# Queries' sweep: the closing product moves from a bank of its own into a shared ring of two, and the transposes of tokens get a fourth bank

## The chip, the cores and the metric

The kernel runs on one core of one Trainium2 chip. The metric is device time in microseconds of one execution; of the kernel before three runs are shown, and one more execution was taken with a profile. Line numbers are those of the kernel before.

## The reference, cut to what matters

One transformer block over 2048 tokens of 1024 features, all in float32. The attention is over the 32 heads of one token, not over tokens.

```python
h = layernorm(x)                                  # 2048 x 1024
q, k, v = (h @ w.T + b for w, b in ((wq, bq), (wk, bk), (wv, bv)))   # as 32 heads of 32
probs = softmax(einsum('shd,std->sht', q, k) / sqrt(32))
x = x + einsum('sht,std->shd', probs, v).reshape(2048, 1024)
y = layernorm(x)
dq1, dq2, dq3 = (nf4_quant_dequant(w) for w in (w1, w2, w3))   # blocks of 64, 16 codes
x = x + (silu(y @ dq1.T) * (y @ dq2.T)) @ dq3.T   # hidden width 2752
```

## The kernel before, in words

The work goes in sweeps: queries (L531 to L560), keys (L623 to L641), values (L713 to L751), then the feed-forward part. Each of the first three projects the 2048 tokens in eight pairs of tiles of 128 tokens. A pair's projection, a product of 256 x 1024 by 1024 x 1024, is done by `products` (L348) with seven block products in place of eight (a scheme of the Strassen-Winograd kind): the left sides are four blocks of tokens (SA11, SA12, SA21, SA22) and four sums of them (S1 to S4, made on VectorE by `differences`, L394), the right sides four blocks of weights and their sums T1 to T4. Each block product is one call of `mm4` (L337): four float32 matmuls that the trace shows as eight rows, into one bank of PSUM.

PSUM has eight banks here. In the queries' sweep they are given out so:

- `z` and `q`, one bank each (pool ps_pj): running sums that several of the seven products add to, and that are copied out in between.
- a ring `x` of two banks (ps_pj, given by `bank`, L301): for `r`, the second product (L371), and for `ptw`, the transposes of weight tiles that `finish` (L147) makes when `flush` lets it go on (L157 to L163).
- `pt`, three banks (pool ps_t, L444): the transposes of token tiles, four transposes of 128 x 128 to a bank (L469 to L471). ScalarE copies each twice, once into A (L474) for the queries and keys, once into V (L475) for the values.
- `y`, one bank, in ps_t too (L385): the closing product, S4 by B22. The queries' sweep passes ps_t to `products` as `apart`; VectorE adds y to the copy u4 of z (L387). In the two later sweeps `apart` is None, and that product is added into z.

The order within a pair is: z and q begin (L362, L365), `fill(7)`, z again (L368), `fill(6)`, r (L372), `fill(2)`, z (L377), `fill(5)`, y (L386), `fill(3)`, q's second product (L389), `fill(4)`. The function `fill` (L539) puts other work between the products: in `fill(5)` the sixteen transposes of the next pair's two token tiles (`transposes`, L467), in `fill(7)` and `fill(3)` a step of a weight tile's transposes, and in each but `fill(5)` a step of the background. After the products a further `flush` follows, then `differences` for the next pair, the layout of the queries (`qk_T`, L401: a transpose and an add of the bias on VectorE) and a chunk of the sums of weights (`weight_chunk`, L509).

The background (L219) quantises the feed-forward weights to 4-bit codes and back: for a tile of weights a chain of fifteen steps, most of them a ScalarE activation `sg` (L242) and a VectorE operation on `r` (L243), with sixteen small scalings by block on ScalarE ahead of it and behind it (L195).

What sets the order: TensorE's instructions are run in the order of the program (L283 puts this engine alone under a schedule by hand). The instructions of VectorE, ScalarE, GpSimd and SyncE are put in order, when the kernel is built, by the framework's planner, from the dependencies, from costs that it assumes, and from the moments at which buffers come free in its plan. The bank that a new tile of a pool takes is chosen there too. On the chip each engine then follows its fixed order.

After the queries' sweep ps_t is closed (L560), and its four banks go to the scores of the keys' sweep (`ps_at`, L568).

Of the kernel before, what the change touches and what calls it, by code (L numbers as in the profile page):

```python
# [12 lines left out]
FP = mybir.dt.float32  # L13
# [3 lines left out]
PSUM = bass.MemoryType.PSUM  # L17

P = 128
# [12 lines left out]
TB = 512  # L32
# [37 lines left out]
def preln_block_kernel(  # L70
# [116 lines left out]
    def flush(steps=3):  # L187
        for _ in range(steps):
            if pending and next(pending[0], flush) is flush:
                pending.pop(0)  # L190
# [69 lines left out]
    def advance(n):  # L260
        for _ in range(n):
            next(bg, None)
# [13 lines left out]
    left, right = ExitStack(), ExitStack()  # L276
# [9 lines left out]
    SA11, SA12, SA22, S1, S2, S3, S4 = range(7)  # L286
# [14 lines left out]
    def bank(nm):  # L301
        pool, tag, bufs = hook["pool"]
        return pool.tile([P, TB], FP, tag=tag, name=nm, bufs=bufs)
# [15 lines left out]
    def load_W(m, name):  # L319
        src = block(m, *RAW[name]) if name in RAW else wtD[m, int(name[1])]  # L320
        nc.sync.dma_start(new_w(name), src)
# [15 lines left out]
    def mm4(dst, w, xop, start, stop):  # L337
        for k in range(4):
            nc.tensor.matmul(  # L339
                dst,  # L340
                w[:, k, :],
                xop[:, k, :],
                start=start and k == 0,
                stop=stop and k == 3,
                skip_group_check=True,
            )

    def products(A, fill, used=lambda name: None, apart=None):  # L348

        def mul(dst, a, w, start, stop):
            mm4(dst, A[:, a], W[w], start, stop)
            used(w)

        def copied(nm, src):
            t = pair.tile([P, TB], FP, tag=nm, name=nm)
            nc.scalar.copy(t, src)  # L358
            return t

        z = ps_pj.tile([P, TB], FP, tag="z", name="z")
        mul(z, SA11, "B11", True, False)  # L362
        g0 = copied("g0", z)
        q = ps_pj.tile([P, TB], FP, tag="q", name="q")
        mul(q, S3, "T3", True, False)  # L365
        s7 = copied("s7", q)
        fill(7)
        mul(z, S2, "T2", False, False)  # L368
        u2 = copied("u2", z)
        fill(6)  # L370
        r = bank("r")  # L371
        mul(r, SA12, "B21", True, True)  # L372
        ce = pair.tile([P, E], FP, tag="C0", name="ce")
        co = pair.tile([P, E], FP, tag="C1", name="co")
        nc.vector.tensor_tensor(ce[:, 0:512], g0, r, ALU.add)
        fill(2)
        mul(z, S1, "T1", False, apart is not None)  # L377
        u4 = copied("u4", z)
        nc.vector.tensor_tensor(co[:, 512:], u4, s7, ALU.add)
        fill(5)  # L380
        if apart is None:
            mul(z, S4, "B22", False, True)
            nc.scalar.copy(ce[:, 512:], z)
        else:
            y = apart.tile([P, TB], FP, tag="y", name="y", bufs=1)  # L385
            mul(y, S4, "B22", True, True)  # L386
            nc.vector.tensor_tensor(ce[:, 512:], u4, y, ALU.add)  # L387
        fill(3)
        mul(q, SA22, "T4", False, True)  # L389
        nc.vector.tensor_tensor(co[:, 0:512], u2, q, ALU.add)  # L390
        fill(4)
        return ce, co
# [8 lines left out]
    def qk_T(t, c, b):  # L401

        nc.vector.transpose(t, c.rearrange("p (h d) -> p h d", d=D))
        nc.vector.tensor_tensor(t, t, b.unsqueeze(2).to_broadcast([P, 32, 32]), ALU.add)
# [36 lines left out]

    sweep = ExitStack()
    work = sweep.enter_context(tc.tile_pool(name="workq", bufs=1, side="right"))
    ps_t = sweep.enter_context(tc.tile_pool(name="ps_t", bufs=3, space=PSUM, side="right"))  # L444

    xt = {}

    def load_x(i):
        xt[i] = work.tile([P, E], FP, tag="x", name="xt", bufs=2)
        nc.sync.dma_start(xt[i], xf[ts(i, P), :])  # L450
# [58 lines left out]
    def weight_chunk(m, k):  # L509

        b = {}
        for nm in ("B11", "B12", "B21", "B22"):
            b[nm] = work.tile([P, TB], FP, tag=f"c{nm}", name=f"c{nm}")
            nc.sync.dma_start(b[nm], block(m, int(nm[1]) - 1, int(nm[2]) - 1)[:, k, :])
        t3 = work.tile([P, TB], FP, tag="cT3", name="cT3")
        nc.vector.tensor_tensor(t3, b["B22"], b["B12"], ALU.subtract)
        nc.vector.tensor_tensor(b["B12"], b["B12"], b["B11"], ALU.subtract)
        nc.vector.tensor_tensor(b["B22"], b["B22"], b["B12"], ALU.subtract)
        nc.vector.tensor_tensor(b["B21"], b["B21"], b["B22"], ALU.subtract)
        for n, t in ((1, b["B12"]), (2, b["B22"]), (3, t3), (4, b["B21"])):  # L520
            nc.sync.dma_start(wtD[m, n][:, k, :], t)

    def next_W(m):
        return lambda name: load_W(m, name)

    def load_A(src, p):
        t = pair.tile([P, 7, 4, P], FP, tag="A", name="A", bufs=2)
        nc.sync.dma_start(t, src[p])
        return t

    for p in range(NP):  # L531
        more = p + 1 < NP
        now = nxt
        if more:
            load_x(2 * p + 2)
            load_x(2 * p + 3)
            nxt = Inputs(p + 1)

        def fill(n):  # L539
            if n in (7, 3):  # L540
                flush(1)
            if n == 5 and more:
                nxt.transposes(0)
                nxt.transposes(1)
            advance(0 if n == 5 else 1)

        cs = products(now.A, fill, (lambda name: None) if more else next_W("k"), ps_t)
        flush(1)
        if more:
            nxt.finished()  # L550
        for j in range(2):
            t = work.tile([P, 32, NH], FP, tag="qd", name="qd", bufs=2)
            qk_T(t, cs[j], qb_sb)
            nc.sync.dma_start(qD[2 * p + j], t)
        now.finished_v()
        weight_chunk("kv"[p // 4], p % 4)
        advance(2)
        if p == NP - 2:
            first = load_A(opD, 0)
# [3 lines left out]
    sweep, sweep_at = ExitStack(), ExitStack()  # L563
# [58 lines left out]
    A = first  # L622
    for p in range(NP):  # L623
        nextA = load_A(opD, p + 1) if p + 1 < NP else load_A(opV, 0)
        qd = load_tiles(qD, p, "ql", 3)

        def fill(n):
            if n in (7, 2, 5, 4):
                part()
            advance(1)  # L630
            if n in (3, 5):
                flush(1)

        cs = products(A, fill, (lambda name: None) if p + 1 < NP else next_W("v"))
        flush(1)
        for j in range(2):
            t = work.tile([P, 32, NH], FP, tag="kd", name="kd", bufs=3)
            qk_T(t, cs[j], kb_sb)
            parts.append(attend(2 * p + j, qd[j], t))
        advance(2)  # L640
        A = nextA  # L641
# [71 lines left out]
    for p in range(NP):  # L713
# [9 lines left out]
        def fill(n):  # L723
# [7 lines left out]
            if n == 3:  # L731
                if p == 0:
                    part()
                elif i + 1 in x1n:
                    keep_T(i + 1, x1n.pop(i + 1))

        cs = products(A, fill, (lambda name: None) if p + 1 < NP else next_op)
        flush(1)
        if p == 0:
            sweep.close()  # L740
            sweep = ExitStack()
# [9 lines left out]
        A = nextA  # L751
# [13 lines left out]
    def op(name, tbp):  # L765
        tag = "T1" if name == "B12" else name
        if ops.get(tag, (None, None))[:2] != (name, tbp):
            load_op(name, tbp)
        return ops[tag][2]
# [24 lines left out]
    def spent(us, finish=True):  # L794
        nonlocal owed
        owed += us * RATE
        n = int(owed)
        owed -= n
        if finish and step["n"] in range(5, 15):
            flush(1)  # L800
        advance(n)
# [75 lines left out]
    class Unit:  # L877


        A = {1: 0, 2: 1, 3: 6, 4: 2, 5: 3, 6: 4, 7: 5}  # L880
# [6 lines left out]
        def mul(self, n, dst, start, stop):  # L887
            mm4(dst, self.w[:, self.A[n]], op(self.B[n], self.tbp), start, stop)
            spent(3.43)
# [203 lines left out]
    now = Unit(*units.pop(0))  # L1093
    now.first()
    for n, (g, tbp) in enumerate(passes):
        half, sides = None, []
        while now is not None and now.tbp == tbp and now.c in g:
# [6 lines left out]
            if g[-1] == NFULL and unit.c == NFULL - 1:  # L1104
# [5 lines left out]
                now = None  # L1110
            if units:
                now = Unit(*units.pop(0))
                now.first()
            if unit.c < PAIRED and unit.c % 2:
                side = Sides(hs[unit.c - 1], n == 0, len(sides))
# [49 lines left out]
```

## Time and profile before

| What | us |
|---|---|
| median of three runs | 2488.63 |
| lowest and highest of them | 2483.4 and 2490.14 |
| profiled execution | 2493.61 |
| its span, first to last instruction | 2491.8 |
| TensorE busy in it | 2388.5 (96%) |
| VectorE busy | 1980.2 (79%) |
| ScalarE busy | 1611.2 (65%) |
| first product of the queries' sweep starts at | 12.8 |
| first product of the keys' sweep starts at | 248.6 |

The profile is of one execution. A group in it is a line of the kernel, an engine, an operation and the tile written and read; so "pt L471" is a transpose of tokens, "y L339" a matmul of the closing product (every block product has the line of `mm4`), and "V L475" ScalarE's copy for the values. Digits in tile names are left out, so A stands for the seven blocks and A21 alike, AV for the tile V and V for V21; wB and wT are weights, u stands for u2 and u4. The mean granted TensorE clock of the span is 0.985 of full speed.

### The profile page before, as it was taken

Reading aid. Unit: us, or ns where it says so; the run is one execution under the profiler, and the core shown is the slowest. Engines: PE = TensorE matmul, PEld = TensorE weight load, DVE = VectorE, ACT = ScalarE, POOL = GpSimd, SP = SyncE. Lnnn points to the kernel's source line nnn. Section 1 sums busy time; section 2 is a strip of 40 time slices with the busy share of each in tenths; the row PEclk is TensorE's granted clock in tenths of the full one; section 3 lists DMA queues with packets and bytes.
Section 4 is the critical chain, followed back from the end, with each engine's and each line's share of the span. In section 5 each row is a group of like instructions: output and inputs, shape, how many; then the busy total and the mean of one; then the engine's idle time right before and its main releaser. Section 6 shows DMA issues by size and latency. Waiting matters only on the chain.

```text
span 2491.8 us, 36722 instructions
## 1 busy us (share of the span) xinstructions
PE 2388.5 (96%) x14000; PEld 1119.1 (45%) x14000; DVE 1980.2 (79%) x2208; ACT 1611.2 (65%) x3267; POOL 278.6 (11%) x352
## 2 busy tenths in 40 slices
PE   7999999999899999999999999999999999999998
PEld 4444455545444444444444444444444444444433
DVE  7999788879988587889989799898988979871022
ACT  3556544344553378898888888889888888871200
POOL 1010000000000012030120301203012030120300
PEclk8999999999999999999999999999999999999998
DMA  8788643656669687394973949739396394862973
GB/s 309 282 313 315 243 156 123 232 211 220 208 230 313 205 287 168 118 191 153 321 171 118 191 147 302 195 110 203 144 301 162 144 198 148 289 153 72 202 269 131
DMA packets 177297, 513.90 MB, mean 206 GB/s; under 512 B 15904, under 2 KB 70176, under 8 KB 154720
## 3 DMA queue, kind: packets, MB, share of 16 engines
q1 hardware_dynamic: 136224, 438.08, 48.1%
q0 software_dynamic: 40320, 73.42, 18.2%
q8 instruction: 110, 1.80, 0.3%
q14 instruction: 67, 0.55, 0.1%
q10 hardware_dynamic: 576, 0.05, 0.0%
HBM read 283.69 MB, written 227.80 MB: 205 GB/s over the span
## 4 chain that ended last, share of the span: by engine, by line
issue 28%; PE 12%; ACT 10%; DVE 10%; DMA 7%; POOL 1%; SPq 0%; DVEq 0%; POOLq 0%; ACTq 0%
DVE r L243 7%; DMA x1d<-acc 5%; PE z L339 4%; ACT sg L242 3%; ACT wn L195 3%; PE z L989 2%; ACT acc L1002 2%; PE q L339 2%; ACT r L195 2%; PE y L989 1%; POOL x1d L1004 1%; PE rr L339 1%; DMA out_dram<-acc 1%; PE r L989 1%; DMA acc<-x1d 1%
## 5 line engine op out<-in xcount | busy, mean ns | idle before, releaser
L243 DVE SCALAR_TENSOR_TENSOR r<-sg,r 128x1024 f32<-128x1024 f32 x780 | 945.8, 1213 | 105.0 <-ACT sg L242 73.6
L242 ACT ACTIVATE sg<-wn 128x1024 f32<-128x1024 f32 x780 | 812.7, 1053 | 313.3 <-DVE r L243 299.2
L1004 POOL DMA_DIRECT2D x1d<-acc x280 | 243.3, 886 | 1283.4 <-ACT acc L1002 1137.3
L339 PE MATMUL z<-xB,w 128*128 128x512 f32 x720 | 323.8, 598 | 3.6 <-ACT u L909 1.9
L339 PE MATMUL z<-xT,w 128*128 128x512 f32 x656 | 295.9, 594 | 4.2 <-ACT u L902 4.2
L339 PE MATMUL q<-xT,w 128*128 128x512 f32 x656 | 291.6, 592 | 0.0
L195 ACT ACTIVATE wn<-wn,rc 128x64 f32<-128x64 f32 x1032 | 267.4, 340 | 22.4 <-DVE rc L215 22.4
L989 PE MATMUL z<-w,h 128*128 128x512 f32 x496 | 236.3, 605 | 21.7 <-ACT acc L1002 18.9
L339 PEld LDWEIGHTS z<-xB,w 128*128 128x128 f32 x720 | 135.0, 191 | 170.3 <-issue 153.8
L339 PEld LDWEIGHTS q<-xT,w 128*128 128x128 f32 x656 | 123.3, 190 | 149.5 <-issue 146.4
L339 PEld LDWEIGHTS z<-xT,w 128*128 128x128 f32 x656 | 122.0, 190 | 151.5 <-issue 138.7
L339 PE MATMUL z<-wT,A 128*128 128x512 f32 x384 | 178.1, 607 | 2.9 <-DVE wT L506 2.0
L339 PE MATMUL q<-wT,A 128*128 128x512 f32 x384 | 173.0, 593 | 1.6 <-DVE A L398 1.6
L339 PE MATMUL z<-wB,A 128*128 128x512 f32 x320 | 152.1, 620 | 13.1 <-ACT u L358 13.1
L195 ACT ACTIVATE r<-r,am 128x64 f32<-128x64 f32 x608 | 154.6, 341 | 13.8 <-DVE r L243 13.5
L989 PEld LDWEIGHTS z<-w,h 128*128 128x128 f32 x496 | 92.4, 192 | 138.6 <-issue 98.3
L989 PE MATMUL y<-w,h 128*128 128x512 f32 x320 | 149.9, 598 | 1.3 <-DVE h L968 1.1
L339 PE MATMUL rr<-xB,w 128*128 128x512 f32 x328 | 147.5, 592 | 0.0
L207 DVE TENSOR_REDUCE am<-wn 128x16 f32<-128x1024 f32 (+1 forms) x65 | 78.3, 1205 | 53.4 <-ACT r L195 47.5
L1002 ACT COPY acc<-z 128x512 f32<-128x512 f32 x160 | 92.8, 581 | 34.6 <-PE z L989 26.3
L339 PEld LDWEIGHTS q<-wT,A 128*128 128x128 f32 x384 | 71.9, 190 | 88.9 <-issue 83.0
L339 PEld LDWEIGHTS z<-wT,A 128*128 128x128 f32 x384 | 71.4, 192 | 83.2 <-issue 80.0
(132 smaller groups left out, 2592.1 us busy)
## 6 DMA issues: line engine op xcount, KB each, us to landing
x1d<-acc POOLq DMA_DIRECT2D x280, 256.0 KB, 6.3
wd<-wop SPq DMA_DIRECT2D x31, 2048.0 KB, 7.6
w<-wd SPq DMA_DIRECT2D x41, 1280.0 KB, 7.8
wn<-in_w_dram SPq DMA_DIRECT2D x63, 512.0 KB, 4.5
xT<-xdT SPq DMA_DIRECT2D x28, 1024.0 KB, 8.9
xB<-xdB SPq DMA_DIRECT2D x24, 1024.0 KB, 6.8
w<-wd SPq DMA_DIRECT2D x42, 512.0 KB, 4.8
w<-wd SPq DMA_DIRECT2D x10, 1536.0 KB, 7.2
```

Source lines behind the costliest of these rows:

```text
L195: nc.scalar.mul(dst[:, ts(n, BLOCK)], src[:, ts(n, BLOCK)], by[:, n : n + 1])
L207: nc.vector.tensor_reduce(am[:, :nb], v.rearrange("p (b e) -> p b e", e=BLOCK), AX.X, ALU.max, apply_absolute_value=True,)
L242: nc.scalar.activation(t, v, AF.Copy, bias=-edge * by, scale=by)
L243: nc.vector.scalar_tensor_tensor(r, t, code, r, ALU.min, ALU.max)
L339: nc.tensor.matmul(dst, w[:, k, :], xop[:, k, :], start=start and k == 0, stop=stop and k == 3, skip_group_check=True,)
L989: nc.tensor.matmul(dst, side[n][:, ts(q, P)], w3T[g[2 * m]][:, W3[n]], start=start and m == 0, stop=stop and m == 1, skip_group_check=True,)
L1002: nc.scalar.copy(t, src)
L1004: nc.gpsimd.dma_start(x1d[8 * tbp + 2 * q + j][n], t, accum_op=ALU.add)
```

## The change

In the queries' sweep the closing product `y` no longer has a bank of its own. It is taken from the ring of two by `bank("y")`, beside r and the weight tiles. The bank that this frees goes to the transposes of tokens: pool ps_t has four `pt` in place of three and no y. `apart` becomes a truth value. Nothing else is changed: the same instructions are issued, and TensorE's are issued in the same order.

```diff
-    def products(A, fill, used=lambda name: None, apart=None):
+    def products(A, fill, used=lambda name: None, apart=False):
...
-        mul(z, S1, "T1", False, apart is not None)
+        mul(z, S1, "T1", False, apart)
...
-        if apart is None:
+        if not apart:
             mul(z, S4, "B22", False, True)
             nc.scalar.copy(ce[:, 512:], z)
         else:
-            y = apart.tile([P, TB], FP, tag="y", name="y", bufs=1)
+            y = bank("y")
             mul(y, S4, "B22", True, True)
             nc.vector.tensor_tensor(ce[:, 512:], u4, y, ALU.add)
...
-    ps_t = sweep.enter_context(tc.tile_pool(name="ps_t", bufs=3, space=PSUM, side="right"))
+    ps_t = sweep.enter_context(tc.tile_pool(name="ps_t", bufs=4, space=PSUM, side="right"))
...
-        cs = products(now.A, fill, (lambda name: None) if more else next_W("k"), ps_t)
+        cs = products(now.A, fill, (lambda name: None) if more else next_W("k"), True)
```

## The prediction

> **What bounds the kernel now.** I first read the page: its busy line says PE 2388.5 of 2491.8 us (96%), so TensorE's own stream sets the end and about 103 us of it is idle. The slices tell where the second engine is full.
>
> ```profile
> PE   7999999999899999999999999999999999999998
> DVE  7999788879988587889989799898988979871022
> PEclk8999999999999999999999999999999999999998
> ```
>
> One slice is 62.3 us. The queries' sweep lies in slices 0 to 3 (12.8 to 248.6 us), and there DVE stands at 9 beside PE. So a wait taken off PE is worth its length only as far as DVE can follow. Second view: who PE waits for up to 260 us (columns: who waits, for whom, total us, times, longest).
>
> ```profile
> PE pt L471 <- ACT V L475: 11.9, 4, 4.2
> PE pt L471 <- DVE xn L334: 4.5, 1, 4.5
> ...
> PE pt L471 <- ACT AV L475: 1.0, 3, 0.3
> ```
>
> The seven waits on ACT's copies out of pt (first and third row) are 12.9 us: the fourth transpose tile of each pair has no bank until a copy empties one of the three. The xn wait is the start, and stays. Third view: PE in order of time, pair 1 and pair 3 (start, us, operation, idle before).
>
> ```profile
> 67.89 1.47 PE L471 MATMUL pt<-ident,xn 128*128 128x128 f32 x12
> 73.58 1.11 PE L471 MATMUL pt<-ident,xn 128*128 128x128 f32 x4 [4.21 <-ACT V L475]
> 74.49 6.10 PE L339 MATMUL y<-wB,A 128*128 128x512 f32 x8
> 80.42 3.60 PE L339 MATMUL q<-wT,A 128*128 128x512 f32 x8
> ...
> 129.22 1.47 PE L471 MATMUL pt<-ident,xn 128*128 128x128 f32 x12
> 131.04 0.65 PE L471 MATMUL pt<-ident,xn 128*128 128x128 f32 x4 [0.34 <-ACT AV L475]
> 131.53 3.60 PE L339 MATMUL y<-wB,A 128*128 128x512 f32 x8
> 134.97 3.60 PE L339 MATMUL q<-wT,A 128*128 128x512 f32 x8
> ```
>
> In pair 1 twelve transposes run, then 4.21 us of nothing, then the last four; and y after them takes 6.10 us where pair 3's takes 3.60. The pause also lowered the clock. Fourth view: stretches with the granted clock.
>
> ```profile
> 60.00:90.00 30.00, 25.79 (x66) 12.21 (x65) 26.69 (x39) 14.43 (x32) 4.04 (x6) 0.89 0.67 249
> ...
> 118.00:145.00 27.00, 26.66 (x78) 12.87 (x77) 26.93 (x39) 13.76 (x30) 3.03 (x4) 1.00 0.75 275
> 145.00:172.00 27.00, 26.66 (x78) 12.69 (x77) 27.00 (x38) 17.82 (x40) 1.77 (x4) 1.00 0.88 324
> ```
>
> Columns: stretch, length, busy us of PE, weight loads, DVE, ACT, POOL, then granted clock, DMA share, GB/s. In pairs 3 and 4, DVE is busy 26.93 and 27.00 of 27: no idle time at all. That is the number that decides this change.
>
> **What the fourth bank removes.** From the first transpose to the start of q's second product, the seven pairs that transpose take 10.66 (36.63 to 47.29), 12.53, 6.73, 5.75, 5.74, 5.75 and 11.17 us: 58.3 us. Without a wait it is 16 transposes at a pitch of 0.109 us (twelve take 1.47, the last 0.27) plus one product of 3.44 us (131.53 to 134.97), 5.18 us, and 36.3 for seven. The whole removable amount is 22.1 us: 12.9 us of waiting, 6.5 us of y at the lower clock (1.5 in pair 0, 2.5 in pair 1, 2.55 in pair 6), and 2.6 us of slow or drained transposes. What is next late on PE itself? In pair 1 u4's copy ends at 71.6 and the copies A at 73.0; without the stall PE wants z's bank and A for pair 2 at 67.9 + 5.2 + 3.4 = 76.5. Those hold by 3.5 us.
>
> The low clock is part of this sum. Here 2.80 us of idle (pair 6) brought y at half speed, 1.32 us (pair 2) did not. [...]
>
> **What the ring of two pays.** Now r, y and the weight tiles' ptw share two banks. A pair asks for r, y and at most two ptw; only six ptw lie in the sweep (111.18, 118.48, 171.61, 188.10, 244.34, 248.22).
> - y needs one free bank. r's add (L375) ends at 154.3 in pair 4 and 180.95 in pair 5, y starts at 157.88 and 184.66: 3.6 us to spare; pair 7 is the tightest, 238.9 against 240.91. Moreover the ring's other bank is mostly free for longer: ptw of 171.61 was copied out at 173.0. Queued behind a waiting y on PE would be everything, but I find no wait: 0.
> - ptw at 188.10 and 244.34 can take r's bank (empty at 180.95, 238.9). ptw at 248.22 needs the bank of y, whose add (L387) ends at 246.57, or that of the ptw before, copied out at 246.21: 1.65 to 2 us to spare. 0; if L387 came 3 us later, about 1.4 us, once.
>
> Bounds for the ring: 0 below, as it frees nothing; above, six ptw and eight y times the longest ring-like wait that the trace has for these groups, 1.4 us (all PE waits for ptw come to 2.1 us in three), 20 us. I take 0, the nearest rows being the gaps just listed. No instruction or DMA is added: eight y's change their bank. The scores' four banks (ps_at) no longer contain y's; the first scores come at about 280 us, far after 246.6: 0.
>
> **What DVE lets through.** TensorE's order is written by hand; ACT, DVE, POOL and SP follow the planner, which lays out the whole program anew when a bank comes free at another moment. The one DVE step with no room is the add that empties q's bank (L390), as the next pair's q waits for it.
>
> ```profile
> 140.65 0.68 DVE L390 TENSOR_TENSOR co<-u,q 128x512 f32<-128x512 f32 x1
> ...
> 166.87 0.68 DVE L390 TENSOR_TENSOR co<-u,q 128x512 f32<-128x512 f32 x1
> ...
> 194.36 0.68 DVE L390 TENSOR_TENSOR co<-u,q 128x512 f32<-128x512 f32 x1
> ```
>
> PE starts the next q at 141.83, 168.18 and 195.41: 0.5, 0.6 and 0.4 us after those ends. PE cannot run ahead of DVE's queue by more. Two ends:
> - *Order unchanged:* DVE gains only the idle that a late y causes, 2.60 us (before L387 at 80.62) and 2.83 (before 220.51), plus the 0.5 of room: 6 us. The other 16 us come back as waits for L390.
> - *Order fully adapted:* DVE also carries the dequantisation (L243 and its kind, 1.2 us each), which runs early: the second job's first step (L234) runs at 90.6 us, while its place in the program is the end of pair 2, about 108 us. So 17 us of DVE work can be put behind the pairs' adds without making anything late: all 22 us.
>
> How much the planner moves depends on the stall in its own plan. Its order of ACT's copies shows one in pairs 0, 1, 2 and 6: three A copies, then V, then AV, so that the three tiles stood ready while ACT was busy; in pairs 3 to 5 it is A, AV, A, AV. Waiting there for at least A and V is about 1.1 us, and u4 not being ready when the sg before it (1.05 us) was placed holds it near 2.5. Four times 1.8 is 7 us that the adds may move ahead of background. Gain: 6 + 7 = **13 us**, between 6 and 22.
>
> **After the sweep** nothing is changed in the program, and PE keeps 80.9 us of idle there (103.3 less 22.4 before 260). The weights for keys are loaded as the last pair's products free them, so they move with PE; DMA is full there (1.01 in 230 to 260), and the loads took 7.6 to 12.4 us of the some 24 between freeing and use. The rest, 1662 us with PE busy 1612, moves as a block. But ACT and DVE may be ordered otherwise there: the waits view holds 13.4 us of z waiting for ACT's u copies (L358, five times) after 260. I take 0 for that and 13 us either way for the range.
>
> **Sum.** The profiled execution took 2493.61 us (span 2491.8); less 13 is 2480.6. The median of the runs shown is 2488.63, 5 us lower, and the same 13 us taken from it give **2475.6 us**.
>
> **Rivals.**
> 1. *DVE holds the line* (0.25): the order hardly changes, PE trades its wait for pt for one on q's bank. 6 us, 2482.6, within 0.3%. For it: DVE at 27.00 of 27. Against: 17 us of early background.
> 2. *All of it arrives* (0.12): 22 us, 2466.6. For it: that same lead; against: pairs 2 to 5, where L390 has half a microsecond.
> 3. *q's bank becomes the stall* (0.21): in the new order one transpose of qd (L403, 1.24), its bias (L404, 1.22) and one L243 (1.22) stand ahead of L390. Less 0.5 of room that is a 3.2 us wait, past the 2.80 at which the clock fell, so 2.5 more: 5.7 us in seven pairs is 40, less 22 is 18 us slower, 2506.6. It decides from a mean L390 delay of about 3.6 us, where wait alone eats 22 us. For it: DVE full; against: L390 stands behind such work today and still comes in time.
>
> The forecast has the remaining 0.42 (2470 to 2481). About 0.3%, 7.5 us, is what a measurement of this kernel can tell from no change. Faster: 0.42 + 0.12 = 0.54; same 0.25; slower 0.21. The range goes from the full gain plus some luck later, 2464, to 2497, the milder part of rival 3 or a gain undone by 13 us of later waits.
>
> **What would show it.** Pt's waits on V and AV gone from PE's list; 16 transposes in one piece; y at 3.6 us in pairs 0, 1 and 6; clock 1.00 in 60 to 90 and 210 to 220. The ring: no wait of y or ptw worth over 1 us. DVE: L390 against the next q tells 13 from 6 or 22, and the start of the keys' first z (248.65 now) reads the sweep's gain directly; I expect about 236. If that start is early and the end is not, the later sweeps gave it back. The prediction is wrong if y waits for a ring bank, or if PE waits for L390 for over 2.8 us.

## The result and the profile after

The changed kernel takes **2493.05 us** (median of ten runs, 2490.31 to 2499.37); ten runs of the kernel before, taken beside them on the same chip, have 2486.64 (2481.87 to 2490.14). The ratio is 1.0028, 95% interval 1.0018 to 1.0038: some 6 us slower, where 13 us faster was forecast. The profiled execution has a span of 2494.2 us and a clock of 0.984.

**In the sweep the mechanism is as forecast.** The slices of the page after:

```profile
DVE  7999688888988597889989798898988989871022
...
PEclk9999899999999999999999999999999999999999
```

The first slice of the clock went from 8 to 9, but the fifth, 249 to 312 us, just behind the sweep, fell from 9 to 8. Whom PE waits for (total, times, longest):

```profile
PE z L339 <- ACT u L358: 16.6, 6, 4.3
...
PE sc L419 <- DMA ql<-qD: 12.6, 1, 12.6
...
PE q L339 <- DVE co L390: 4.0, 3, 2.6
```

No row for `pt` on V or AV is left and none for `y`. PE waits for L390 4.0 us, in three. The waits of z on u were 13.4 us in five and are 16.6 in six. The second row is new: the first scores of the keys' sweep wait 12.6 us for the queries' tile `ql`. PE in order of time, pair 1, then q of pair 3, then the first product of the keys' sweep:

```profile
62.62 1.91 PE L471 MATMUL pt<-ident,xn 128*128 128x128 f32 x16
64.36 3.60 PE L339 MATMUL y<-wB,A 128*128 128x512 f32 x8
...
130.36 5.40 PE L339 MATMUL q<-wT,A 128*128 128x512 f32 x8 [2.58 <-DVE co L390]
...
234.37 3.60 PE L339 MATMUL z<-wB,A 128*128 128x512 f32 x8
```

Sixteen transposes run in one piece, y takes 3.60 us, and the keys' sweep begins 14.3 us earlier (248.65 before). The stretch of pair 1 and 2 (length, busy us of PE, weight loads, DVE, ACT, POOL, clock, DMA share, GB/s) has PE full at full clock:

```profile
60.00:90.00 30.00, 30.00 (x94) 15.03 (x93) 28.19 (x41) 15.62 (x34) 3.26 (x6) 1.00 0.66 248
```

**Behind the sweep it is given back.** I call *sweep* the time from the first product of the queries to the first of the keys, and *hand-over* the time from there to the second group of scores (L419) of the keys' first pair. Before, in that stretch:

```profile
268.08 3.70 PE L339 MATMUL z<-wB,A 128*128 128x512 f32 x8 [2.10 <-ACT u L358]
282.01 1.78 PE L419 MATMUL sc<-kd,ql 32*32 32x32 f32 x128
290.79 1.77 PE L419 MATMUL sc<-kd,ql 32*32 32x32 f32 x128
```

After:

```profile
255.59 6.60 PE L339 MATMUL z<-wB,A 128*128 128x512 f32 x8 [3.71 <-ACT u L358]
...
285.04 1.80 PE L419 MATMUL sc<-kd,ql 32*32 32x32 f32 x128 [12.56 <-DMA ql<-qD]
286.78 4.67 PE L339 MATMUL z<-wT,A 128*128 128x512 f32 x8
...
294.81 1.77 PE L419 MATMUL sc<-kd,ql 32*32 32x32 f32 x128
```

The hand-over grew from 42.14 (290.79 less 248.65) to 60.44 us (294.81 less 234.37), by 18.3. Its parts in these two profiles: 14.2 of waiting (12.56 + 3.71 - 2.10) and 3.9 of products at the lower clock (6.60 and 4.67 in place of 3.70). So the second scores come 4.0 us *later*, though the sweep ended 14.3 us earlier.

Who is late? SP's queue, before and then after (start, us, DMA issues of a line, out<-in):

```profile
208.82 5.10 SPq L514 DMA_DIRECT2D cB<-in_wvT_dram  x4
...
229.64 0.73 SPq L321 DMA_DIRECT2D wB<-in_wkT_dram  x1
...
255.71 1.73 SPq L521 DMA_DIRECT2D wtDv<-cB  x2
...
262.86 0.93 SPq L618 DMA_DIRECT2D ql<-qD  x2
```

```profile
220.38 0.59 SPq L321 DMA_DIRECT2D wB<-in_wkT_dram  x1
...
234.95 0.53 SPq L321 DMA_DIRECT2D wT<-wtDk  x1
...
243.22 3.93 SPq L514 DMA_DIRECT2D cB<-in_wvT_dram  x4
249.29 0.33 SPq L528 DMA_DIRECT2D A<-opD  x1
270.41 2.06 SPq L521 DMA_DIRECT2D wtDv<-cB  x2
...
274.98 1.67 SPq L618 DMA_DIRECT2D ql<-qD  x3
```

L514 loads the last chunk of weights for the values (`weight_chunk`), L521 stores its sums, L618 loads ql. Before, the chunk's loads are issued ahead of the seven weights of keys (L321, 229.6 to 248.4); after, behind them, 34 us later, into DMA engines that are full (share 1.01 to 1.04 from 220 to 260 us). They take 11.8 to 13.6 us to land. Then the sums wait in VectorE's fixed order: behind the final add of the keys' first pair (L390), which itself waits for PE's q, and between steps of background (L243):

```profile
265.65 0.69 DVE L390 TENSOR_TENSOR co<-u,q 128x512 f32<-128x512 f32 x1 [1.85 <-PE q L339]
266.26 1.22 DVE L243 SCALAR_TENSOR_TENSOR r<-sg,r 128x1024 f32<-128x1024 f32 x1
267.39 0.69 DVE L516 TENSOR_TENSOR cT<-cB,cB 128x512 f32<-128x512 f32 x1
268.55 1.23 DVE L243 SCALAR_TENSOR_TENSOR r<-sg,r 128x1024 f32<-128x1024 f32 x1 [0.47 <-ACT sg L242]
269.70 0.69 DVE L517 TENSOR_TENSOR cB<-cB,cB 128x512 f32<-128x512 f32 x1
```

SP's waits hold the row that ties this together: `SPq L521 <- DVE cB L517: 19.8, 1, 19.8`. For 19.8 us SP stood at a store: some nine until the chunk's own loads had landed, eleven for VectorE. The loads of ql stood behind that store. They don't wait for it by themselves: on another queue (ql_pool, below) they go out 12.7 us ahead of it. In the last ten of the wait the DMA engines idled (share 0.10 and 0.00 in the last but one column), and VectorE (third of the busy times) was not full:

```profile
260.00:265.00 5.00, 5.00 (x11) 2.20 (x10) 3.66 (x3) 2.78 (x8) 0.00 (x0) 0.85 0.10 40
265.00:270.00 5.00, 5.00 (x13) 2.28 (x12) 3.87 (x5) 4.65 (x14) 0.00 (x0) 1.00 0.00 0
```

### The profile page after: what moved, and what is told of

Same layout as the page of the kernel before. It is cut to its first block, busy times and chain, and to the rows that moved or that the text cites. A ratio compares the mean times of both kernels' runs of the same rounds, so it can differ in the third digit from the quotient of the medians.

```text
span 2494.2 us, 36701 instructions
## 1 busy us (share of the span) xinstructions
PE 2384.4 (96%) x14000; PEld 1116.6 (45%) x14000; DVE 1981.0 (79%) x2208; ACT 1611.6 (65%) x3267; POOL 276.7 (11%) x352
## 4 chain that ended last, share of the span: by engine, by line
issue 24%; PE 13%; ACT 12%; DVE 12%; DMA 6%; POOL 1%; SPq 0%; DVEq 0%; POOLq 0%; ACTq 0%
DVE r L243 8%; PE z L339 5%; DMA x1d<-acc 4%; ACT sg L242 4%; ACT wn L195 3%; PE z L989 2%; ACT acc L1002 2%; ACT r L195 2%; PE q L339 2%; PE y L989 1%; PE rr L339 1%; PE po L1058 1%; POOL x1d L1004 1%; PE r L989 1%; ACT wop L162 1%
## 5 line engine op out<-in xcount | busy, mean ns | idle before, releaser
L243 DVE SCALAR_TENSOR_TENSOR r<-sg,r 128x1024 f32<-128x1024 f32 x780 | 945.5, 1213 | 105.1 <-ACT sg L242 74.8
L195 ACT ACTIVATE wn<-wn,rc 128x64 f32<-128x64 f32 x1032 | 267.5, 341 | 18.5 <-DVE rc L215 18.5
L339 PE MATMUL z<-wB,A 128*128 128x512 f32 x320 | 155.9, 633 | 15.3 <-ACT u L358 15.3
L195 ACT ACTIVATE r<-r,am 128x64 f32<-128x64 f32 x608 | 154.4, 341 | 15.4 <-DVE r L243 15.1
## 6 DMA issues: line engine op xcount, KB each, us to landing
x1d<-acc POOLq DMA_DIRECT2D x280, 256.0 KB, 6.0
```

The lines of the kernel that those rows point to most:

```text
L195: nc.scalar.mul(dst[:, ts(n, BLOCK)], src[:, ts(n, BLOCK)], by[:, n : n + 1])
L243: nc.vector.scalar_tensor_tensor(r, t, code, r, ALU.min, ALU.max)
L339: nc.tensor.matmul(dst, w[:, k, :], xop[:, k, :], start=start and k == 0, stop=stop and k == 3, skip_group_check=True,)
```

## The experiments

**Theory:** the bank gains its share in the sweep; VectorE, ScalarE and SP don't follow PE by as much, and the last weight chunk, met late at the hand-over, takes the gain back. **Rivals:** the ring of two costs something; a transfer is late for lack of bandwidth; the background on VectorE or ScalarE alone is what holds the hand-over; one profile's scatter. Four to twelve runs each; times in us. A ratio is to runs of the kernel before that were taken beside that row's on the same chip; their medians lie between 2486.5 and 2489.0, so it is not the quotient of two medians of this table. "_before" is the same edit in the kernel before.

| kernel | median | ratio [95%] | sweep | hand-over |
|---|---|---|---|---|
| before | 2486.64 | 1 | 235.87 | 42.14 |
| after | 2493.05 | 1.0028 [1.0018, 1.0038] | 221.80 | 60.44 |
| after_again | 2492.69 | 1.0021 [1.0012, 1.0030] | 221.96 | 58.85 |
| ring_alone | 2487.84 | 0.9997 [0.9988, 1.0007] | 231.86 | 42.13 |
| chunk_early | 2490.62 | 1.0014 [1.0005, 1.0023] | 221.95 | 56.82 |
| chunk_early_before | 2487.44 | 0.9998 [0.9989, 1.0007] | 231.71 | 42.16 |
| ql_pool | 2488.99 | 1.0011 [1.0002, 1.0020] | 220.66 | 54.68 |
| light_after | 2472.48 | 0.9940 [0.9921, 0.9959] | 217.65 | 44.77 |
| light_before | 2486.30 | 0.9992 [0.9980, 1.0004] | 231.58 | 41.61 |
| noact_after | 2490.05 | 1.0000 [0.9987, 1.0012] | 220.82 | 54.56 |
| nodve_after | 2479.55 | 0.9961 [0.9944, 0.9978] | 219.38 | 48.90 |
| nodve_before | 2479.06 | 0.9955 [0.9940, 0.9970] | 227.07 | 41.49 |
| pool_after | 2493.08 | 1.0019 [1.0006, 1.0033] | 235.86 | 43.74 |
| pool_before | 2513.05 | 1.0102 [1.0080, 1.0123] | 256.01 | 42.14 |
| held | 2485.84 | 0.9980 [0.9967, 0.9993] | 220.81 | 49.57 |
| held_before | 2491.20 | 1.0009 [0.9996, 1.0023] | 231.31 | 46.97 |
| held_early | 2484.18 | 0.9972 [0.9962, 0.9983] | 221.37 | 48.87 |
| moved | 2482.59 | 0.9975 [0.9964, 0.9987] | 225.73 | 45.16 |
| moved_before | 2492.98 | 1.0020 [1.0009, 1.0032] | 240.97 | 41.88 |
| held_moved | 2487.92 | 1.0001 [0.9989, 1.0012] | 230.39 | 46.25 |

Sweep and hand-over are of one profiled execution each.

**ring_alone**: y in the ring, three banks for the transposes.

```diff
-    ps_t = sweep.enter_context(tc.tile_pool(name="ps_t", bufs=4, space=PSUM, side="right"))
+    ps_t = sweep.enter_context(tc.tile_pool(name="ps_t", bufs=3, space=PSUM, side="right"))
```

> Half of the change: y moves into the ring of two, pt keeps three banks, one bank lies idle. Every engine's order is then the one of the kernel before. Theory (the loss sits in the hand-over to the keys' sweep, where the last weight chunk came late and held SP's queue in front of the queries' tiles; the ring is free): as before, 2486.6 us within 4, pt still waits some 12 us, no wait of y or ptw over 1 us, first scores near 282 us. Rival ring (the shared banks cost the time): slower by 4 to 7 us, with waits of y or ptw on r's add or on ACT's copy of wop.

Measured: ratio 0.9997, hand-over as before, the same waits for pt (12.4 us on V), none for y or ptw. The ring costs nothing that can be measured; that rival falls. The order of VectorE's and ScalarE's work, and of SP's as far as the hand-over, is also that of before, so this profile serves as a second one of it.

**after_again**: the changed kernel once more, nothing edited.

> The changed kernel once more, for a second profile of the same program. Theory: again the keys' first product at 233 to 236 us, a wait of the first scores for ql of 10 to 15 us, second scores at 291 to 296, time 2490 to 2496. Rival (the waits of the first profile were chance): the wait for ql is under 5 us.

Measured: 12.7 us for ql again, hand-over 58.85. With chunk_early_before, whose orders are before's too (SP's but for one load), there are three profiles of before's kind (sweep 235.87, 231.86, 231.71, mean 233.1; hand-over 42.1 each) and two of after's (means 221.9 and 59.6). So the **sweep gains 11.3 us and the hand-over loses 17.5**; net 6.2 lost, and the medians say 6.4. Profiles of one order differ by up to 4.2 us in the sweep, but the hand-over's loss is there in both of after's. Scatter of one profile is not the cause.

**chunk_early and chunk_early_before**: the last chunk's loads are issued ahead of the last pair's products.

```diff
-        t3 = work.tile([P, TB], FP, tag="cT3", name="cT3")
+        yield; t3 = work.tile([P, TB], FP, tag="cT3", name="cT3")
...
-        cs = products(now.A, fill, (lambda name: None) if more else next_W("k"), True)
+        chunk = weight_chunk("kv"[p // 4], p % 4); more or next(chunk); cs = products(now.A, fill, (lambda name: None) if more else next_W("k"), True)
...
-        weight_chunk("kv"[p // 4], p % 4)
+        list(chunk)
```

> The changed kernel, with the last pair's four chunk loads issued ahead of its products, so ahead of the keys' weights in SP's queue. Theory: the wait of the first scores for ql (12.6 us) falls under 3, the first scores start at 270 to 275 us in place of 285.0, and the time falls by 9 to 14 us against the changed kernel, to about 2481 (5 less than before). Rival DVE (the sweep's 14 us were only lent, since DVE was full from 33 to 280 us and makes the first keys no earlier whatever SP does): the first scores wait as long for kd's bias add (L404) as they waited for ql, start at 280 to 285, and the time stays at 2490 to 2494.

> The same edit on the kernel before, whose last chunk was loaded ahead of the keys' weights anyway. Theory: no change, 2486.6 us within 4, first scores near 282 us. Rival (the early load is worth something by itself, whatever the banks): faster by 5 us or more.

Measured: the wait for ql is gone and the first scores start at 273.15, 11.9 us earlier than after's. Yet the ratio is only 0.07 to 0.14% under the two of after (some 2 to 3.5 us), and the intervals overlap. PE in the hand-over of chunk_early:

```profile
273.15 1.79 PE L419 MATMUL sc<-kd,ql 32*32 32x32 f32 x128 [0.77 <-DVE kd L404]
...
281.52 6.64 PE L339 MATMUL z<-wT,A 128*128 128x512 f32 x8 [6.58 <-ACT g L358]
...
291.53 1.78 PE L419 MATMUL sc<-kd,ql 32*32 32x32 f32 x128
```

A new wait stands in the old one's place: z's bank is copied out by ScalarE's g (L358). In ScalarE's order that copy, at 280.90, stands behind background work (six scalings L195 at 279.46, and three sg from 275.47), which itself waited 4.66 us for VectorE's L243. ScalarE there:

```profile
275.47 1.06 ACT L242 ACTIVATE sg<-wn 128x1024 f32<-128x1024 f32 x1 [4.66 <-DVE r L243]
...
279.46 1.54 ACT L195 ACTIVATE r<-r,am 128x64 f32<-128x64 f32 x6 [0.27 <-DVE r L243]
280.90 0.56 ACT L358 COPY g<-z 128x512 f32<-128x512 f32 x1
```

So the late chunk is one part; background that stands ahead of the copies PE needs is another. In the kernel before, the same edit changes nothing (0.9998).

**ql_pool**: the keys' first ql loads on GpSimd's queue, not SP's.

```diff
-            nc.sync.dma_start(t, src[2 * p + j])
+            (nc.gpsimd if tag == "ql" and p == 0 else nc.sync).dma_start(t, src[2 * p + j])
```

> The changed kernel, with the first pair's two loads of ql on GpSimd's queue, so that nothing on SP's queue stands ahead of them; the last chunk stays late. Theory in its narrow form (only SP's queue ahead of ql): the scores' wait falls from 12.6 to under 2 and the time by about 11 us. Theory in its wide form (the late chunk also keeps DVE's sums L516 to L519 in front of kd's transposes L403): the scores then wait for kd's bias until 280 us, so the wait falls from 12.6 to 7 or 8 and the time by 4 to 5. Rival (DMA is saturated there): ql lands no earlier than 284 us and nothing changes.

Measured: no ql wait; the first scores start at 277.59 after 7.29 us of waiting for VectorE's kd (L404), and the ratio falls by 0.10 to 0.17% (2.5 to 4 us; the intervals overlap). The issue of ql on GpSimd's queue, then the store that still holds SP:

```profile
255.50 1.32 POOL L618 DMA_DIRECT2D ql<-qD  x2 [61.23 <-DMA cB<-in_wvT_dram]
```

```profile
268.23 2.06 SPq L521 DMA_DIRECT2D wtDv<-cB  x2
```

The loads of ql themselves waited for a load of the chunk (cB, from in_wvT_dram) to land, so here a late chunk holds them on another queue too; SP goes on to its store only 12.7 us later. VectorE's order is that of after, instruction by instruction, which makes this the narrowest of the experiments. SP's blocked queue is real, and behind it VectorE is nearly as late: of the 12.56 us, 7.3 stay when ql is there.

**light_after and light_before**: steps 1 to 6 of the first eight weight tiles of the background are left out.

```diff
-                if i == 0:
-                    nc.vector.tensor_scalar(r, v, edge, code, ALU.is_lt, ALU.mult)
+                if n < 8 and 1 <= i <= 6: pass
+                elif i == 0: nc.vector.tensor_scalar(r, v, edge, code, ALU.is_lt, ALU.mult)
```

> The changed kernel with less background: for the first eight weight tiles, steps 1 to 6 of the fifteen are left out (six VectorE and five ScalarE operations a tile, some 58 us of VectorE in all, so those tiles' codes are not the reference's). New theory (VectorE's queue is the line from 33 to 280 us: it is full of background that runs ahead, so what PE gains in the sweep it must wait off in the first pair of keys, whatever wait is taken away there): with VectorE relieved the sweep's gain stays, first scores at 262 to 270 us, and this kernel is 10 to 20 us faster than light_before. Rival (structure: the order of SP's queue and the memory shared with the queries' tiles hold the first scores, VectorE does not): first scores still 3 us or more behind light_before's, and the time not under light_before's by more than 3.

> The kernel before with the same steps left out, as the measure for light_after. Theory: pt still waits on ACT's copies for 6 us or more in the sweep, first scores at 275 to 282 us, time 2476 to 2487. Rival: as the theory, since both differ only in light_after.

Measured: with less background the change is worth 13.8 us (2472.48 against 2486.30), what was forecast for the full kernel. The hand-over is 44.8, the ql wait 2.2. In light_before PE still waits 12.9 us for pt, and the kernel gains nothing from the lighter background.

**noact_after and nodve_after, nodve_before**: of the same tiles' first steps only ScalarE's activations, or only VectorE's operations, are left out.

```diff
-                    nc.scalar.activation(t, v, AF.Copy, bias=-edge * by, scale=by)
+                    (n < 8 and i <= 5) or nc.scalar.activation(t, v, AF.Copy, bias=-edge * by, scale=by)
```

```diff
-                    nc.vector.scalar_tensor_tensor(r, t, code, r, ALU.min, ALU.max)
+                    (n < 8 and i <= 5) or nc.vector.scalar_tensor_tensor(r, t, code, r, ALU.min, ALU.max)
```

(In noact_after VectorE reads v in place of the activation's result.)

> The changed kernel; for the first eight weight tiles ScalarE's activations of steps 1 to 5 are left out and VectorE's steps read the weights in their place (40 activations of 1.05 us less; VectorE's load is the same; those codes are not the reference's). Which engine's background holds the keys' first pair? If VectorE's load is the line (theory): little changes, 2485 to 2493, second scores at 288 to 295 us. If ScalarE's queue is (rival: its copies u and g stand behind activations and scalings): as in light_after, 2472 to 2480, second scores at 275 to 282.

> The counterpart: for the first eight weight tiles VectorE's steps 1 to 5 are left out, ScalarE's activations stay (40 operations of 1.21 us less on VectorE; those codes are not the reference's). Theory (VectorE's load is the line): as in light_after, 2470 to 2480, second scores at 272 to 283 us. Rival (ScalarE's queue): 2485 to 2493.

> The kernel before with VectorE's steps 1 to 5 left out for the first eight weight tiles, as the measure for nodve_after (2479.6). Theory (VectorE's background takes the gain of the banks and costs the kernel before next to nothing): within 3 us of before, so nodve_after is 5 us or more faster. Rival (the steps left out are worth 8 us by themselves): 2482 or less.

Measured: of the 18.3 us that the hand-over has over before's, leaving out ScalarE's part takes 5.9, VectorE's 11.5, both (light_after) 15.7. That points to VectorE, but the control missed: nodve_before was expected within 3 us of before and came 0.45% faster. Its waits for pt shrink to 9.8 us and its sweep to 227.1, so the pair is equal (sweep gains 7.7, hand-over loses 7.4). VectorE's load thus acts on both sides, and nodve doesn't say by itself what the banks are worth. Nor does it fit with light_before, which leaves out more and gains nothing: each such edit also brings a new plan of all four planned engines, and no run separates the two.

**pool_after and pool_before**: the four sums of a weight chunk run on GpSimd.

```diff
-        nc.vector.tensor_tensor(t3, b["B22"], b["B12"], ALU.subtract)
+        nc.gpsimd.tensor_tensor(t3, b["B22"], b["B12"], ALU.subtract)
```

(L516 to L519, all four alike.)

> The changed kernel with the four sums of each weight chunk on GpSimd (nothing left out): VectorE is relieved of 8 times 2.7 us in the sweep, 22 us. New theory (VectorE's queue is the line): half or more of what was lost in the first pair of keys comes back, first scores at 268 to 278 us, 6 us or more faster than the changed kernel: 2480 to 2487. Rival (structure): GpSimd is slower at it, so the last chunk comes later still, the scores' wait for ql grows past 12.6 and the time is 2493 or more.

> The kernel before with the sums of the chunks on GpSimd. New theory: PE hardly waits for VectorE there today, the pt waits on ACT stay, so 2486 within 5. Rival (structure): the same, or slower where the last chunk is late here too.

Measured: pool_after is as slow as after, pool_before some 26 us slower than before. The sweep of pool_after is 235.86, with 15.4 us of waits for L390, the forecast's third rival in part. Its hand-over, 43.74, is near before's, but PE also reaches the keys as late as before (248.64), so this doesn't show that it was the sums on VectorE that held it. In pool_before the sweep is 256.0: PE waits 17.7 us for pt, 4.9 once for u and 3.7 for L390.

VectorE wasn't relieved as expected. In pool_before, GpSimd's sums of one chunk, then VectorE in the same time:

```profile
62.35 1.59 POOL L517 TENSOR_TENSOR cB<-cB,cB 128x512 f32<-128x512 f32 x1
64.03 2.13 POOL L518 TENSOR_TENSOR cB<-cB,cB 128x512 f32<-128x512 f32 x1
66.23 1.59 POOL L519 TENSOR_TENSOR cB<-cB,cB 128x512 f32<-128x512 f32 x1
```

```profile
62.75 2.28 DVE L238 SCALAR_TENSOR_TENSOR r<-wn,r 128x1024 f32<-128x1024 f32 x1
64.95 1.75 DVE L396 TENSOR_TENSOR AV<-V,AV 128x512 f32<-128x512 f32 x1
66.62 2.28 DVE L243 SCALAR_TENSOR_TENSOR r<-sg,r 128x1024 f32<-128x1024 f32 x1
68.83 0.68 DVE L397 TENSOR_TENSOR AV<-AV 128x512 f32<-128x512 f32 x1
69.43 1.21 DVE L243 SCALAR_TENSOR_TENSOR r<-sg,r 128x1024 f32<-128x1024 f32 x1
```

Beside a sum, L243 takes 2.28 us in place of 1.21. Added up over the sweep, VectorE's steps that overlap a sum take 22 us longer than their like in pool_before, and 18 us in pool_after: about the 22 us that were to be saved. From 33 to 230 us VectorE was busy 188.4 us in pool_before and 190.9 in pool_after, 186.9 in before, which has the sums on VectorE. So the pair says nothing of what a relieved VectorE would do; why the loss in the sweep is so much larger in the kernel before was not settled.

**held and held_before**: the planner may order the background's next steps only after the layout's last bias add of the pair (L404), until the keys' second pair (later, only the two steps at each keys' pair's end).

```diff
-        nc.vector.tensor_tensor(t, t, b.unsqueeze(2).to_broadcast([P, 32, 32]), ALU.add)
+        hook["hold"] = nc.vector.tensor_tensor(t, t, b.unsqueeze(2).to_broadcast([P, 32, 32]), ALU.add).ins
...
-        for _ in range(n):
-            next(bg, None)
+        with tc.issue_after(hook["hold"]) if hook.get("hold") else ExitStack():
+            [next(bg, None) for _ in range(n)]
...
-        advance(2)
+        advance(2); p >= 1 and hook.pop("hold")
```

> The changed kernel, whole, with the run-ahead of the background cut: VectorE's background steps that the program writes after a pair's last bias add (L404) stay behind it in VectorE's order, from the queries' first pair to the keys' second. Theory: q's bank, the last chunk and the first keys come earlier on VectorE, the queries' gain stays, second scores at 270 to 282 us, 8 to 18 us faster than the changed kernel: 2475 to 2485, so faster than both. Rival (all of VectorE's work up to there must be done anyway, or weights come late for it): the waits move to ptw or to the feed-forward weights, 2488 or more.

> The kernel before with the same bound on the background, as the measure for held. Theory: the pt waits on ACT's copies are the cost there and mostly stay, some shrink with the background's activations moved back: 2480 to 2490, and held is 4 us or more faster. Rival (the bound alone is worth the time, the banks nothing): as fast as held.

Measured: the hand-over falls from 59.6 to 49.6, with 5.4 us for ql left; held is 0.20% faster than before. In the kernel before, the same hold costs 4.8 us of hand-over (PE waits 3.8 for g) and gains nothing. The same banks are worth +0.25% without the hold (the mean of after's two ratios) and -0.29% with it (0.9980 over 1.0009).

**held_early**: held and chunk_early together.

> The held kernel with the last chunk's loads ahead of the keys' weights as in chunk_early (whole computation). Theory (two causes in a row: VectorE's background, then SP's queue behind the late last chunk): the remaining wait of the first scores for ql, 5.4 us in held, falls under 2, second scores at 274 to 278 us (282.97 in held), and the time is 3 to 8 us under held: 2477 to 2483, the fastest whole version. Rival (whatever wait is taken away there, another of its size follows, as in chunk_early): second scores at 281 to 285 and the time within 2 us of held's 2485.8.

Measured: 0.9972. Neither ql nor g is waited for; a transfer is next:

```profile
264.05 6.74 PE L339 MATMUL z<-wB,A 128*128 128x512 f32 x8 [4.88 <-DMA A<-opD]
```

In held_early DMA is full from 220 to 265 us (share 1.01 to 1.05 in stretches of 10 us up to 260, 1.00 in the last five; 341 to 423 GB/s). A is issued at 250.12 and lands 14 us later, so here, unlike for ql in after, full DMA engines stand ahead of PE.

**moved and moved_before**: the last chunk is made in the second pair, with chunk 1, and none in the last.

```diff
-        weight_chunk("kv"[p // 4], p % 4)
+        [weight_chunk("kv"[c // 4], c % 4) for c in ((1, 7) if p == 1 else (p,) if more else ())]
```

> The changed kernel, whole, with the last weight chunk (1 MB loaded, 1 MB stored, four VectorE sums) done in the second pair beside that pair's own, so not at the hand-over. Theory (the hand-over to the keys loses the sweep's gain to three things that are full there: SP's queue behind the chunk, VectorE's and ScalarE's background, the DMA engines at 400 GB/s): the wait for ql falls under 3 us, keys' start to second scores takes 48 to 55 us (60.4 in the changed kernel, 42.1 before), time 2484 to 2490. Rival (the background alone decides, a moved chunk only moves the wait): 56 us or more, 2490 or more.

> The kernel before with the chunk moved so. Theory: PE comes late enough there for all three, so the stretch stays at 41 to 43 us and the time at 2486 within 4. Rival (moving the chunk is worth something by itself): 2481 or less.

Measured: with the whole background in place, moving one chunk brings the hand-over to 45.16, 15.3 us less than after's, and the time to 0.9975. PE in moved:

```profile
123.61 1.94 PE L471 MATMUL pt<-ident,xn 128*128 128x128 f32 x8 [7.62 <-DVE xn L334]
...
274.79 1.78 PE L419 MATMUL sc<-kd,ql 32*32 32x32 f32 x128
283.56 1.78 PE L419 MATMUL sc<-kd,ql 32*32 32x32 f32 x128
```

No idle time stands before either group of scores; of the hand-over's waits one on u (3.42 us) is left. PE reaches the keys 4.0 us later than in after (238.40), which is part of the 15.3; the second scores come 11.3 us earlier. The price is a new wait in pair 3, where VectorE normalises the tokens late (7.62 us); four sums of the second chunk stand among those steps, 2.7 us. In the kernel before, the same edit is 0.20% slower: the chunk was not late there, the hand-over stays, and the pt waits grow from 12.9 to 17.2 us. So **where the last chunk is made decides the sign of the change**: +0.25% with it in the last pair, -0.45% with it in the second (0.9975 over 1.0020). What the pair doesn't separate is the chunk from the new plan that comes with it: of VectorE's first 500 instructions only 302 stand in moved where they stand in after (all 500 in ql_pool, 468 in chunk_early).

**held_moved**: both.

> The changed kernel with the background held back as in held and the last chunk moved as in moved (whole computation). Theory (with SP and VectorE free what is left in held_early is the DMA engines, full from 220 to 270 us; 2 MB less there is 5 us at 400 GB/s): the wait for A, 4.9 us in held_early, falls under 2, the stretch takes 43 to 46 us, time 2477 to 2482, faster than every whole version so far. Rival (the DMA engines are not the limit, or the added sums in the second pair cost what is won): the stretch takes 48 or more, or the keys start 4 us later, and the time is 2483 or more.

Measured: 1.0001, worse than moved and no better than held. The wait for A is gone, as it should be if the full DMA engines had made it; but the xn wait of 8.0 us stays, g is waited for 3.8 us, and the sweep is 230.4. The two remedies don't add. The fastest whole kernels are held_early and moved, 0.28% and 0.25% faster than before with intervals that overlap.

## Why the prediction was wrong

- **The banks: right.** The pt waits went, y is at 3.60 us, the clock is 1.00 in 60 to 90, and ring_alone shows the ring to be free, as forecast.
- **What VectorE lets through: right in kind, 13 forecast, 11.3 measured.** The single profiles say 14, the mean over three and two says 11.3. That 13 came so near is partly luck: no run tells its halves, 6 and 7, apart. PE waits for L390 in three places, 4.0 us in all and 2.58 at most, so the prediction's own sign (over 2.8 us) is met by the sum and not by any single wait. The third rival's price (5.7 us in each of seven pairs) was neared once, by 2.58 us and q at 5.40.
- **The step that failed: "After the sweep".** It said of the weights for keys that they "move with PE", and of a new order there: "I take 0". The weights did move with PE; in after no product waits for them. But I treated the rest as a block that starts earlier, and the block I had measured, 1662 us, begins only at 830 us; apart from the slack of the weights, the keys' sweep had no term but that zero. Three things have to be ready at the hand-over besides the weights: the last chunk's sums and stores, ql, and the copies out of z. SP's queue had the chunk's loads behind the keys' weights and ql behind the chunk's stores; VectorE had the sums behind L390 and background. The term was 17.5 us, outside the 13 that I had allowed either way, and it alone turns the sign.
- **The cause.** Shown: the sweep's gain is lost in the hand-over, in both profiles of after. Shown: SP's blocked queue is the first of the waits there, and when it is taken away another takes its place at once (ql_pool, chunk_early). Shown: the change turns from a loss into a gain when the last chunk is made elsewhere (moved) or the background is held back (held), each with its control, and most of the hand-over's loss goes in either case where the chunk is moved or background is left out (15.3 of 18.3 us in moved, 15.7 in light_after). So it isn't one late load, but the fixed orders of SP, VectorE and ScalarE meeting a PE that comes 11 us sooner. VectorE was not full at that point (3.66 and 3.87 of 5 us from 260 to 270); its sums stood behind an add that waited for PE. Not shown: how much of what moved and held gain is the new plan as such. That the planner put the chunk's loads behind the keys' weights *because* of its own view of the fourth bank is argued from the orders of the two traces; its plan itself was not looked at.
- **The slower rival** that I named (q's bank) was not the one that came. I looked for it inside the changed sweep. The way to find the other stood in the profile of before: DVE at 9 and DMA full from 230 us, SP loading ql at 262.86, 19 us ahead of the first scores, behind stores of the same queue.

Open: why the sweep of pool_before loses so much more than that of pool_after; why the sweep of held_moved is longer than either parent's; and the last 2 to 3 us of the hand-over's loss, which stay in moved and light_after.

## What to carry to other kernels

A wait taken away in one stage is worth what the *next* stage can take in early: list every queue that must have delivered at the seam (loads, stores, sums, copies out), with its slack in the trace, and charge the gain for each that is shorter than it. In after SP issued the loads of ql (274.98 us) only behind the store at which it had stood for 19.8 us (270.41), so look for a store that waits for a busy engine ahead of a load that is wanted soon. If such a change comes out slower, move the one late piece of work before giving the change up: here moving one weight chunk turned +0.25% into -0.25%.

## What the runs showed of the hardware

- SP stood 19.8 us at a store, and the loads behind it stood too; in the last ten of these microseconds the DMA engines ran at 0 to 10%. Full DMA engines (share 1.01 to 1.05 and 335 to 428 GB/s in stretches of 10 us of after, held_early and moved) and idle ones look alike in a list of waits; here the window view told them apart.
- Idle gaps of 1.98 us (held), 2.57 us (chunk_early) and 2.58 us (after) were followed by q at 5.40 us; gaps of 1.32 us (before), 2.57 us (noact_after) and 3.71 us (after_again) by products of 3.60 to 3.70 us, and the 3.71 us of after by one of 6.60. So a gap's length alone doesn't settle the clock. In the traces of before and after each stretch at the lower clock, apart from the last, which the end of the trace cuts, is at half clock (0.50) and lasts 3.41, 6.83 or 13.65 us (131.75 to 135.16, 254.63 to 261.45 and 275.11 to 288.76 in after).
- A 128x512 float32 sum (L517) took 0.68 us on VectorE (before); on GpSimd, whose spans are rough, 1.26 to 2.13 us in pool_before and 1.60 to 2.18 us in pool_after. Steps of VectorE slowed too: in pool_before, beside a sum, L243 took 2.28 us in place of 1.21 and L396 1.75 us in place of 0.68.
